# A state-space layer at VectorE's pace: the norm and the batch statistics move to ScalarE and TensorE

## The chip, the cores and the metric

The kernel runs on one core of a Trainium2 chip. A core has five engines that work side by side, each through its own list of instructions in order: TensorE (PE, with its weight loads shown apart as PEld), VectorE (DVE), ScalarE (ACT), GpSimd (POOL) and SyncE (SP), which here issues the transfers. They meet only through semaphores. The metric is the device time of one execution in microseconds.

## The reference

A network of four layers works on an image batch of 4 x 96 x 64 x 64. The change lies in layer 0, two Mamba blocks one after the other with a batch norm at the end:

```python
for i in range(2):
    mu  = seq.mean(-1); var = ((seq - mu) ** 2).mean(-1)
    h   = (seq - mu) * rsqrt(var + EPS) * ln_g + ln_b          # the norm over the 96 channels
    xs, z = split(h @ in_w)
    xc  = silu(causal conv of 4 taps over xs)
    dt, Bm, Cm = split(xc @ xproj_w)
    delta = softplus(dt @ dt_w + dt_b)
    dA, dBx = exp(delta * A), delta * Bm * xc                   # 192 channels x 16 states
    hstates = scan over the tokens of (h = dA * h + dBx)
    y   = (sum over states of hstates * Cm + Dp * xc) * silu(z)
    seq = seq + y @ out_w
out = fus_w @ [seq, pooled] + fus_b
out = (out - mean(out)) * rsqrt(var(out) + EPS) * bn_g + bn_b   # per channel, over batch and pixels
```

Layers 1 to 3 (a convolution block, an attention and a Fourier block with small feed-forward parts) are the same before and after.

## The kernel before

The tokens of each image, 4096, are cut into 4 stretches of 1024. An *item* is one image, one stretch and one of the two blocks, 32 items in all, ordered so that each image's state is carried from stretch to stretch (`items`: stretch, then block i, then image b, so four items of block 0 alternate with four of block 1).

An item has 24 *tiles* of 128 x 1024, each 4 states of 32 channels. For each tile ACT makes dA (`exp`, L455), DVE makes u = delta·xc·B (L471) and the scan (L475), POOL multiplies with C (`times_c`, L481), and PE sums over the states into `y` (`sum_y`, L500). The tiles of `pool_tiles` = 2, 5, 7, 10, 13, 15, 18, 21 divide the work otherwise: POOL makes u (`times_b`, L461), and ACT writes dA into PSUM (`dap`). For the other tiles PE spreads B's rows over the partitions (`rep`, L195: operand x, while u goes to a second buffer). All of x, u and `dap` share one ring of two PSUM buffers (`psum_x`), so `rep` and `dap` of a tile wait until the one or two tiles before are through on DVE.

The order is written out by hand: under `manual_schedule` each engine executes its instructions in the order in which the loop over m (one step for a tile, called a slot below) names them. In a slot stand, in this order: the scan, `rep` or `exp` for the next tile, `exp` three tiles ahead, `times_c`, `keep_state`, `times_b`, the y work, `load_x`, `project`, `finish`, `keep_stats`, and last what `first_stage` has put into the slot. `first_stage(k)` prepares item k while the items before it are scanned; its slot numbers are relative, and modulo 24 they say in which slot of a phase (24 tiles) its work stands. What matters here, with lines:

- slot 13 (-11): item's x is loaded, POOL puts the 3 tokens of the item before into `n` (L266, L268)
- slot 17 (-7): PE subtracts the channel mean with a 96 x 96 matrix `center` (L274), channels on the partitions
- slot 18 (-6): ACT squares (L280) and copies to `n` (L281)
- slot 19 (-5): PE sums the squares over the channels with `ones` (L287), which also spreads the sum over the partitions
- slot 20 (-4): ACT makes the reciprocal root by Ln and Exp (L292, L293)
- slot 21 (-3): DVE multiplies it into `n` (L299), POOL keeps the last 3 tokens (L301)
- slots 22 to 1: matmuls of the convolution from `n` (`spread`, L205), slots 0, 1, 3: ACT copies them out (L309), then Silu
- slot 12: softplus of delta on ACT (L357), with a load of its function table before and one after it (L222)
- slots 12, 13, 13: three matmuls for z (L205, w_z); slots 13, 14, 14: ACT copies them out (L309); slot 19: Silu of z (L383), with two table loads
- the item that has just been scanned: slot 15 `project` (L518, L219) on PE, slot 17 `finish` on ACT (L527 for block 0, L529 for block 1), slot 18 `keep_stats` on DVE (L537, two bn_stats, block 1 alone)

The PSUM tiles of `tile_ps` (L274, L287, the convolution, z, delta, `project`) share another ring of two buffers. A matmul into such a tile waits until ACT has emptied the tile two before it.

Of the kernel before, what the change touches and what calls it, by code (L numbers as in the profile page):

```python
# [9 lines left out]
F32 = mybir.dt.float32  # L10
# [3 lines left out]
AF = mybir.ActivationFunctionType  # L14
ALU = mybir.AluOpType
# [3 lines left out]
B, C, HW, L = 4, 96, 64, 4096  # L19
NT = B * L  # L20
T = 1024
NSC = L // T
MB = 512
# [27 lines left out]
class Net:  # L51
# [20 lines left out]
    def consts(self, ctx):  # L72
        tc, nc, ins = self.tc, self.nc, self.ins
        pool = ctx.enter_context(tc.tile_pool(name="const", bufs=1))
        self.cpool = pool
        self.vec = pool.tile([C, NV96], F32, name="vec")
        nc.sync.dma_start(self.vec, ins["vec96"])
        self.vec128 = pool.tile([128, NV128], F32, name="vec128")
        nc.sync.dma_start(self.vec128, ins["vec128"])
        self.ones = pool.tile([C, C], F32, name="ones")  # L80
        nc.vector.memset(self.ones, 1.0)
        self.eps = pool.tile([128, 1], F32, name="eps")
        nc.vector.memset(self.eps, EPS)
# [4 lines left out]
        self.stats = pool.tile([C, NT // MB, 6], F32, name="stats")  # L88
        self.osc = pool.tile([C, 1], F32, name="osc")
        self.osh = pool.tile([C, 1], F32, name="osh")  # L90


    def layer0(self, dram, scratch):
        tc, nc, ins = self.tc, self.nc, self.ins
        x_in = ins["x"]
        with ExitStack() as ctx:
            cp = ctx.enter_context(tc.tile_pool(name="l0c", bufs=1))
# [17 lines left out]
            w_z = cp.tile([C + 1, 2, DIN], F32, name="w_z")  # L115
# [11 lines left out]
            gpw = load(cp, "gpw", [C, C])  # L127
            nega = cp.tile([128, 48], F32, name="nega")
            fbias = cp.tile([C, B], F32, name="fbias")
            pooled = cp.tile([C, B * NSC], F32, name="pooled")  # L130

            with tc.tile_pool(name="l0s", bufs=1) as wk:
# [9 lines left out]
                for a in range(0, 2 * 4 * DIN, MB):  # L142
                    ps = small(C + 1, MB)
# [6 lines left out]
                for i in range(2):  # L150
# [4 lines left out]
                    ps = small(C + 1, HID)  # L155
# [33 lines left out]
            def tile_ps(rows=C):  # L189
                return psum.tile([128, MB], F32, name="ps", tag="ps")[:rows]  # L190
# [54 lines left out]
            def load_x(b, s, i):  # L245
                x = wk.tile([C, T], F32, name="x", tag="x", bufs=2)
                nc.sync.dma_start(x, xd[:, b] if i else x_in[b, :, s * T : (s + 1) * T])
                return x

            def first_stage(k):  # L250
# [5 lines left out]
                def at_slot(t):  # L256
                    def keep(f):
                        steps.setdefault(t - 24, []).append(f)

                    return keep  # L260

                @at_slot(-11)
                def _():
                    m["xn"] = load_x(b, s, i)
                    if s == 0:
                        nc.gpsimd.memset(n[:, :3], 0.0)  # L266
                    else:
                        nc.gpsimd.tensor_copy(n[:, :3], halo[:, b, i])  # L268

                @at_slot(-7)  # L270
                def _():
                    m["ps"] = [tile_ps(), tile_ps()]
                    for at, ps in zip(halves, m["ps"]):
                        nc.tensor.matmul(ps, self.center, m["xn"][:, at], start=True, stop=True)  # L274

                @at_slot(-6)
                def _():
                    m["sq"] = wk.tile([C, T], F32, name="sq", tag="sq")
                    for at, ps in zip(halves, m["ps"]):
                        nc.scalar.activation(m["sq"][:, at], ps, AF.Square)  # L280
                        nc.scalar.copy(n[:C, 3 + at.start : 3 + at.stop], ps)  # L281

                @at_slot(-5)
                def _():
                    m["ps"] = [tile_ps(), tile_ps()]
                    for at, ps in zip(halves, m["ps"]):
                        nc.tensor.matmul(ps, self.ones, m["sq"][:, at], start=True, stop=True)  # L287

                @at_slot(-4)
                def _():  # L290
                    for ps in m["ps"]:
                        nc.scalar.activation(ps, ps, AF.Ln, scale=1.0 / C, bias=self.eps[:C])  # L292
                        nc.scalar.activation(ps, ps, AF.Exp, scale=-0.5)  # L293

                @at_slot(-3)
                def _():
                    for at, ps in zip(halves, m["ps"]):
                        x = n[:C, 3 + at.start : 3 + at.stop]
                        nc.vector.tensor_mul(x, x, ps)  # L299
                    if s < NSC - 1:  # L300
                        nc.gpsimd.tensor_copy(halo[:, b, i], n[:, T:])  # L301

                def parts_of(name, ws, rhs, slots, bufs):

# [52 lines left out]
                    nc.scalar.activation(m["delta"], m["delta"], AF.Softplus)  # L357
                    exp_set()

                parts_of("z", [(w_z[:, i], 3)], n, ((12, 13), (13, 14), (13, 14)), 3)  # L360

                @at_slot(13)
                def _():
# [14 lines left out]
                for p in range(3):  # L378
                    at_slot(14 + 3 * p)(lambda p=p: du(p))

                @at_slot(19)
                def _():
                    nc.scalar.activation(m["z"], m["z"], AF.Silu)  # L383
                    exp_set()
# [148 lines left out]
            def keep_stats(k):  # L533
                b, s, i = items[k]
                a = b * L + s * T
                for at in halves:
                    nc.vector.bn_stats(self.stats[:, (a + at.start) // MB, :], made[k]["x"][:, at])  # L537


            b_slots = {2: 5, 4: 7, 7: 10, 9: 13, 12: 15, 15: 18, 18: 21, 23: NTL + 2}  # L540
# [1 line left out]
            with tc.manual_schedule(engines=engines):  # L542
                gp = global_pool()
                stages = [first_stage(k) for k in range(len(items))]
                first = min(stages[0])
                for m in range(first, last + 19):
                    k, t = divmod(m, NTL)
                    if 0 <= m < last:
                        scan(m, *xu)
                    if 0 <= m + 1 < last:  # L550
                        if on_pool(m + 1):
                            exp(m + 1)
                        elif (t + 1) % NTL in group_starts:
                            xu = rep(m + 1)
                    if 0 <= m + AHEAD < last and not on_pool(m + AHEAD):
                        exp(m + AHEAD)
                    if 1 <= m <= last:
                        times_c(m - 1)
                    if 3 <= m < last + 3:
                        keep_state(m - 3)  # L560
                    if -1 <= m and t in b_slots and m - t + b_slots[t] < last:
                        times_b(m - t + b_slots[t])
                    for k0 in range(max(k - 1, 0), min(k + 1, len(items))):
                        at = m - NTL * k0
                        for p in range(3):
                            if at == 8 * p + 3:
                                start_y(k0, p)

                            if at - 8 * p in (4, 6, 8, 10):
                                sum_y(k0, at - 4)  # L570
                            if at == 8 * p + 11:
                                gate(k0, p)
                        if at == 34:
                            made[k0]["x"] = load_x(*items[k0])
                        if at == 39:
                            project(k0)
                        if at == 41:
# [844 lines left out]
```

## Time and profile before

The time is 4223.3 us, the median of 3 runs (4220.02 to 4226.23). Layer 0 ends at about 2724 us of the profiled 4222.8. Busy time from 200 to 2600 us, the steady part of layer 0:

| engine | busy us of 2400 | share |
|---|---|---|
| POOL | 2288.6 | 95% |
| DVE | 2283.8 | 95% |
| PE | 1745.9 | 73% |
| ACT | 1579.2 | 66% |

The instructions that the change touches, over the whole layer (count by mean duration):

| line | engine, what | count | ns |
|---|---|---|---|
| L274 | PE, centre, records of 96x512 | 128 | 643 |
| L280, L281 | ACT, square and copy, 96x512 | 64 each | 598, 580 |
| L287 | PE, sum of squares | 128 | 620 |
| L292, L293 | ACT, Ln and Exp, 96x512 | 64 each | 644, 574 |
| L309 z | ACT, z's copies, 128x512 | 96 | 580 |
| L383 | ACT, Silu of z, and table loads | 32 | 1486, 1283 each load |
| L529 | ACT, finish of block 1 | 32 | 673 |

In such a table the time of a PE instruction is a record of the profile; a matmul in f32 leaves two records. The durations contain the time in which an instruction overlaps its neighbour, so the distance of two starts is shorter: two copies of 0.58 us start 0.48 us apart.

### The profile page before, as it was taken

The numbers are of one execution on the slowest core, as the hardware profiler recorded it, in microseconds if no ns is written. First come the engines' busy times: TensorE is split into PE (matmuls) and PEld (weight loads), VectorE is DVE, ScalarE is ACT, GpSimd is POOL, SyncE is SP. The second block draws the span as 40 slices with busy tenths as digits, with TensorE's granted clock in tenths as the row PEclk, the third lists the DMA queues.
The fourth block names the chain that finished last, engine by engine and source line by source line (L and its number), as shares of the span: only waits on it lengthen the run. The fifth ranks groups of instructions, "written<-read, shape, count | busy, mean of one in ns | idle before, by whom it ended". The sixth has DMA issues, their size and how long they took to land. (4 is left out here: it accounts for less than half of the span.)

```text
span 4222.8 us, 42511 instructions
## 1 busy us (share of the span) xinstructions
PE 3233.2 (77%) x13088; PEld 1310.8 (31%) x13088; DVE 3189.6 (76%) x2474; ACT 2514.7 (60%) x4098; POOL 2997.8 (71%) x1651
## 2 busy tenths in 40 slices
PE   6677677777767777776777776579999888887987
PEld 2111112111211211121121111277445436555642
DVE  4999999999999999999999999731222583444649
ACT  4666666666666666666666665322555575544547
POOL 1999999999999999999999999611110264333418
PEclk8788888888878888888888887669999998899989
DMA  7557566566656656665665666363000000001111
GB/s 171 136 149 172 132 155 162 139 147 158 164 136 152 161 137 147 161 161 137 151 161 137 147 158 165 77 202 130 0 0 1 1 1 5 23 28 28 44 43 53
DMA packets 183276, 468.02 MB, mean 111 GB/s; under 512 B 53108, under 2 KB 55134, under 8 KB 179968
## 3 DMA queue, kind: packets, MB, share of 16 engines
q1 hardware_dynamic: 183048, 465.31, 43.6%
q8 instruction: 103, 1.69, 0.2%
q14 instruction: 125, 1.02, 0.1%
HBM read 391.62 MB, written 73.50 MB: 110 GB/s over the span
## 5 line engine op out<-in xcount | busy, mean ns | idle before, releaser
L481 POOL TENSOR_TENSOR hs<-hs,crep 128x1024 f32<-128x1024 f32 x768 | 1799.2, 2359 | 108.1 <-DVE hs L475 55.0
L475 DVE TENSOR_TENSOR_SCAN hs<-da,state,u 128x1024 f32<-128x1024 f32 x384 | 901.7, 2348 | 24.9 <-DVE u L471 0.5
L455 ACT ACTIVATE dap<-ddb,nega 128x1024 f32<-128x1024 f32 x256 | 286.3, 1118 | 722.0 <-DVE u L471 721.6
L471 DVE TENSOR_TENSOR u<-udb,rep 128x1024 f32<-128x1024 f32 x512 | 627.7, 1226 | 72.3 <-PE rep L195 40.2
L455 ACT ACTIVATE da<-ddb,nega 128x1024 f32<-128x1024 f32 x512 | 583.7, 1143 | 67.7 <-DVE hs L475 65.7
L195 PE MATMUL rep<-r,sel_bq 96*128 96x512 bf16 x576 | 226.8, 485 | 514.4 <-DVE hs L475 505.9
L461 POOL TENSOR_TENSOR up<-udb,brep 128x1024 f32<-128x1024 f32 x256 | 605.3, 2365 | 4.7 <-DMA ud<-du 4.7
L500 PE MATMUL y<-hs,sel_r 128*32 128x512 f32 x3072 | 501.9, 724 | 4.6 <-POOL hs L481 4.6
L475 DVE TENSOR_TENSOR_SCAN hs<-dap,state,up 128x1024 f32<-128x1024 f32 x192 | 447.1, 2329 | 16.4 <-ACT dap L455 16.4
L205 PE MATMUL ps<-n,w_x 97*64 97x512 f32 x1536 | 424.7, 680 | 10.9 <-DVE n L299 10.8
L475 DVE TENSOR_TENSOR_SCAN hs<-da,u 128x1024 f32<-128x1024 f32 x128 | 293.0, 2289 | 8.1
L195 PEld LDWEIGHTS <-sel_bq 96*128 96x128 bf16 x576 | 39.1, 103 | 780.2 <-DVE hs L475 582.2
L1002 POOL CAST hq<-y 128x512 fp8e5<-128x512 f16 x192 | 118.5, 641 | 222.1 <-DVE y L1001 222.1
L205 PEld LDWEIGHTS ps<-n,w_x 97*64 97x64 f32 x1536 | 152.2, 155 | 287.3 <-issue 217.6
L205 PE MATMUL ps<-n,w_z 97*64 97x512 f32 x384 | 121.1, 714 | 129.3 <-ACT z L309 116.2
L1150 POOL TENSOR_TENSOR av<-av,ec 128x780 f32<-128x780 f32 x32 | 58.8, 1838 | 197.3 <-ACT av L1147 197.3
L796 POOL TENSOR_TENSOR xc<-xc,rs 96x512 f32<-96x512 f32 x32 | 40.4, 1266 | 209.8 <-ACT rs L795 163.8
L500 PEld LDWEIGHTS y<-hs,sel_r 128*32 128x32 f32 x3072 | 65.6, 116 | 319.1 <-issue 167.8
L219 PE MATMUL ps<-xc,xproj 64*102 64x512 f32 x384 | 152.1, 952 | 3.5 <-ACT xc L320 3.5
L475 DVE TENSOR_TENSOR_SCAN hs<-dap,up 128x1024 f32<-128x1024 f32 x64 | 145.3, 2270 | 7.6 <-ACT dap L455 5.7
L373 POOL TENSOR_TENSOR du<-delta,xc 128x512 f32<-128x512 f32 x96 | 122.6, 1277 | 32.1 <-ACT delta L357 22.3
L1147 ACT ACTIVATE av<-xr_ps,vec 128x65 f32<-128x65 f32 x384 | 117.0, 424 | 47.5 <-PE xr_ps L1135 47.5
(255 smaller groups left out, 6067.3 us busy)
## 6 DMA issues: line engine op xcount, KB each, us to landing
ddb<-dd SPq DMA_DIRECT2D x768, 128.0 KB, 3.3
udb<-ud SPq DMA_DIRECT2D x768, 128.0 KB, 4.4
crep<-cd SPq DMA_DIRECT2D x512, 128.0 KB, 4.0
brep<-cd SPq DMA_DIRECT2D x256, 128.0 KB, 3.6
dd<-delta SPq DMA_DIRECT2D x64, 384.0 KB, 3.9
ud<-du SPq DMA_DIRECT2D x192, 128.0 KB, 3.2
band<-in_band SPq DMA_DIRECT2D x24, 1024.0 KB, 4.8
gt<-in_idft SPq DMA_DIRECT2D x64, 256.0 KB, 2.7
```

The costliest lines, as they stand in the source:

```text
L195: nc.tensor.matmul(ps[:, at], w, rhs[:, at_in], start=start, stop=stop, **kw)
L205: nc.tensor.matmul(ps[rows], w[:, 64 * p : 64 * p + 64], rhs[:, at.start + shift : at.stop + shift], start=k == 0, stop=k == len(ws) - 1, ...
L219: nc.tensor.matmul(ps, w[rows, p], x[rows, p], start=start and p == 0, stop=p == 2)
L373: nc.gpsimd.tensor_mul(u, m["delta"][:, of], m["xc"][:, of])
L455: nc.scalar.activation(da, made[k]["dd", h, j], AF.Exp, scale=nega[:, col : col + 1])
L461: nc.gpsimd.tensor_mul(u, made[k]["ud", h, j], made[k]["brep", g])
L471: nc.vector.tensor_mul(u, made[k]["ud", h, j], x)
L475: nc.vector.tensor_tensor_scan(hs[:, 1:], made[k].pop(("da", t)), u, 0.0 if s == 0 else st, ALU.mult, ALU.add)
L481: nc.gpsimd.tensor_mul(hs[:, :T], hs[:, 1:], made[k]["crep", order[t][1]])
L500: nc.tensor.matmul(made[k]["y", p][row : row + 32], sel_r, made[k]["hs", t][:, at], start=False, stop=True, skip_group_check=True,)
L1002: nc.gpsimd.tensor_copy(q[:, m, :], y2, saturate=False)
L1147: nc.scalar.activation(v[:, k, d], xr[:, at], AF.Identity, scale=self.v128(w, cg + d), bias=self.v128(bias, cg + d))
```

## The change

The norm is made with the tokens on the partitions. PE takes pieces of 128 tokens of x as the stationary operand and `center` as the moving one, so that the centred values come out as 128 tokens x 96 channels. There the sum of squares over the channels is a sum along the free axis, which ACT's Square gives as its accumulator output; the reciprocal root is one value for each token, on 128 x 8 instead of 96 x 1024, and ACT multiplies it in as a scale for each partition. PE then turns the pieces back with the identity matrix, and ACT copies them into `n`. DVE's multiply is gone; POOL's two small copies of three tokens go to ACT (a memset at the start of each image stays on POOL).

The batch statistics were DVE's bn_stats. Now ACT's `finish` gives the sum of each piece as its accumulator output, and a second ACTIVATE gives the sum of squares, shifted by the mean of the first piece. The end of the layer makes mean and variance of these sums.

To make room on ACT, the copies of z come a slot later (14, 15, 15; the third z matmul in slot 14 instead of 13), and Silu of z moves from slot 19 to 16.

```diff
                 @at_slot(-7)
                 def _():
-                    m["ps"] = [tile_ps(), tile_ps()]
-                    for at, ps in zip(halves, m["ps"]):
-                        nc.tensor.matmul(ps, self.center, m["xn"][:, at], start=True, stop=True)
+                    m["ps"] = [tile_ps(128), tile_ps(128)]
+                    for q in range(8):
+                        nc.tensor.matmul(
+                            m["ps"][q // 4][:, q % 4 * C : q % 4 * C + C],
+                            m["xn"][:, q * 128 : q * 128 + 128],
+                            self.center,
...
                 @at_slot(-6)
                 def _():
-                    m["sq"] = wk.tile([C, T], F32, name="sq", tag="sq")
-                    for at, ps in zip(halves, m["ps"]):
-                        nc.scalar.activation(m["sq"][:, at], ps, AF.Square)
-                        nc.scalar.copy(n[:C, 3 + at.start : 3 + at.stop], ps)
+                    m["nt"] = wk.tile([128, 8, C], F32, name="nt", tag="nt")
+                    m["rs"] = wk.tile([128, 8], F32, name="rs", tag="rs")
+                    for q in range(8):
+                        nc.scalar.activation(
+                            m["nt"][:, q],
+                            m["ps"][q // 4][:, q % 4 * C : q % 4 * C + C],
+                            AF.Square,
+                            accum_out=m["rs"][:, q : q + 1],
+                        )
+                    nc.scalar.activation(m["rs"], m["rs"], AF.Ln, scale=1.0 / C, bias=self.eps)
+                    nc.scalar.activation(m["rs"], m["rs"], AF.Exp, scale=-0.5)
...
                 @at_slot(-5)
                 def _():
-                    m["ps"] = [tile_ps(), tile_ps()]
-                    for at, ps in zip(halves, m["ps"]):
-                        nc.tensor.matmul(ps, self.ones, m["sq"][:, at], start=True, stop=True)
+                    for q in range(8):
+                        x = m["ps"][q // 4][:, q % 4 * C : q % 4 * C + C]
+                        nc.scalar.mul(m["nt"][:, q], x, m["rs"][:, q : q + 1])
...
                 @at_slot(-4)
                 def _():
-                    for ps in m["ps"]:
-                        nc.scalar.activation(ps, ps, AF.Ln, scale=1.0 / C, bias=self.eps[:C])
-                        nc.scalar.activation(ps, ps, AF.Exp, scale=-0.5)
+                    m["ps"] = [tile_ps(), tile_ps()]
+                    for q in range(8):
+                        nc.tensor.matmul(
+                            m["ps"][q // 4][:, q % 4 * 128 : q % 4 * 128 + 128],
+                            m["nt"][:, q],
+                            self.ident,
...
                 @at_slot(-3)
                 def _():
+                    if s == 0:
+                        nc.gpsimd.memset(n[:, :3], 0.0)
+                    else:
+                        nc.scalar.copy(n[:, :3], halo[:, b, i])
                     for at, ps in zip(halves, m["ps"]):
-                        x = n[:C, 3 + at.start : 3 + at.stop]
-                        nc.vector.tensor_mul(x, x, ps)
+                        nc.scalar.copy(n[:C, 3 + at.start : 3 + at.stop], ps)
                     if s < NSC - 1:
-                        nc.gpsimd.tensor_copy(halo[:, b, i], n[:, T:])
+                        nc.scalar.copy(halo[:, b, i], n[:, T:])
...
-                parts_of("z", [(w_z[:, i], 3)], n, ((12, 13), (13, 14), (13, 14)), 3)
+                parts_of("z", [(w_z[:, i], 3)], n, ((12, 14), (13, 15), (14, 15)), 3)
...
-                @at_slot(19)
+                @at_slot(16)
                 def _():
                     nc.scalar.activation(m["z"], m["z"], AF.Silu)
                     exp_set()
...
-                    else:
-                        nc.scalar.activation(o[:, at], ps, AF.Identity, bias=fbias[:, b : b + 1])
+                        continue
+                    a = (b * L + s * T + at.start) // MB
+                    nc.scalar.activation(
+                        o[:, at], ps, AF.Identity, bias=fbias[:, b : b + 1], accum_out=self.sums[:, a : a + 1]
+                    )
+                    if (b, s, at.start) == (0, 0, 0):
+                        nc.vector.tensor_scalar_mul(self.shift, self.sums[:, :1], 1.0 / MB)
+                        nc.vector.tensor_scalar(sbias, fbias, self.shift, None, ALU.subtract)
+                    nc.scalar.activation(
+                        ps, ps, AF.Square, bias=sbias[:, b : b + 1], accum_out=self.squares[:, a : a + 1]
+                    )
...
-                        if at == 42 and items[k0][2]:
-                            keep_stats(k0)
...
-            nc.vector.bn_aggr(mv, self.stats)
+            for k, x in enumerate((self.sums, self.squares)):
+                nc.vector.reduce_sum(mv[:, k : k + 1], x, axis=mybir.AxisListType.X)
+            nc.vector.tensor_scalar_mul(mv, mv, 1.0 / NT)
+            nc.vector.tensor_sub(d, mv[:, :1], self.shift)
+            nc.vector.tensor_mul(d, d, d)
+            nc.vector.tensor_sub(mv[:, 1:2], mv[:, 1:2], d)
```

More of the change, by code (lines that the diff above doesn't have):

```diff
@@ L87, in consts @@
         nc.vector.tensor_scalar_add(self.center, self.ident[:C, :C], -1.0 / C)
-        self.stats = pool.tile([C, NT // MB, 6], F32, name="stats")
+        self.sums = pool.tile([C, NT // MB], F32, name="sums")
+        self.squares = pool.tile([C, NT // MB], F32, name="squares")
+        self.shift = pool.tile([C, 1], F32, name="shift")
         self.osc = pool.tile([C, 1], F32, name="osc")
@@ L129, in layer0 @@
             fbias = cp.tile([C, B], F32, name="fbias")
+            sbias = cp.tile([C, B], F32, name="sbias")
             pooled = cp.tile([C, B * NSC], F32, name="pooled")
@@ L264, in _ @@
                     m["xn"] = load_x(b, s, i)
+                @at_slot(-7)
+                def _():
+                    m["ps"] = [tile_ps(128), tile_ps(128)]
[4 more added lines that the diff above has]
+                            self.center,
+                            start=True,
+                            stop=True,
+                        )
+                @at_slot(-6)
+                def _():
+                    m["nt"] = wk.tile([128, 8, C], F32, name="nt", tag="nt")
[9 more added lines that the diff above has]
+                    nc.scalar.activation(m["rs"], m["rs"], AF.Exp, scale=-0.5)
+                @at_slot(-5)
+                def _():
+                    for q in range(8):
+                        x = m["ps"][q // 4][:, q % 4 * C : q % 4 * C + C]
+                        nc.scalar.mul(m["nt"][:, q], x, m["rs"][:, q : q + 1])
+                @at_slot(-4)
+                def _():
+                    m["ps"] = [tile_ps(), tile_ps()]
[4 more added lines that the diff above has]
+                            self.ident,
+                            start=True,
+                            stop=True,
+                        )
+                @at_slot(-3)
+                def _():
                     if s == 0:
@@ L267, in _ @@
                     else:
-                        nc.gpsimd.tensor_copy(n[:, :3], halo[:, b, i])
-                @at_slot(-7)
-                def _():
-                    m["ps"] = [tile_ps(), tile_ps()]
+                        nc.scalar.copy(n[:, :3], halo[:, b, i])
                     for at, ps in zip(halves, m["ps"]):
-                        nc.tensor.matmul(ps, self.center, m["xn"][:, at], start=True, stop=True)
-                @at_slot(-6)
-                def _():
-                    m["sq"] = wk.tile([C, T], F32, name="sq", tag="sq")
-                    for at, ps in zip(halves, m["ps"]):
-                        nc.scalar.activation(m["sq"][:, at], ps, AF.Square)
-                        nc.scalar.copy(n[:C, 3 + at.start : 3 + at.stop], ps)
-                @at_slot(-5)
-                def _():
-                    m["ps"] = [tile_ps(), tile_ps()]
-                    for at, ps in zip(halves, m["ps"]):
-                        nc.tensor.matmul(ps, self.ones, m["sq"][:, at], start=True, stop=True)
-                @at_slot(-4)
-                def _():
-                    for ps in m["ps"]:
-                        nc.scalar.activation(ps, ps, AF.Ln, scale=1.0 / C, bias=self.eps[:C])
-                        nc.scalar.activation(ps, ps, AF.Exp, scale=-0.5)
-                @at_slot(-3)
-                def _():
-                    for at, ps in zip(halves, m["ps"]):
-                        x = n[:C, 3 + at.start : 3 + at.stop]
-                        nc.vector.tensor_mul(x, x, ps)
+                        nc.scalar.copy(n[:C, 3 + at.start : 3 + at.stop], ps)
                     if s < NSC - 1:
-                        nc.gpsimd.tensor_copy(halo[:, b, i], n[:, T:])
+                        nc.scalar.copy(halo[:, b, i], n[:, T:])
                 def parts_of(name, ws, rhs, slots, bufs):
@@ L527, in finish @@
                         nc.scalar.copy(o[:, at], ps)
-                    else:
-                        nc.scalar.activation(o[:, at], ps, AF.Identity, bias=fbias[:, b : b + 1])
+                        continue
+                    a = (b * L + s * T + at.start) // MB
+                    nc.scalar.activation(
+                        o[:, at], ps, AF.Identity, bias=fbias[:, b : b + 1], accum_out=self.sums[:, a : a + 1]
+                    )
+                    if (b, s, at.start) == (0, 0, 0):
[3 more added lines that the diff above has]
+                        ps, ps, AF.Square, bias=sbias[:, b : b + 1], accum_out=self.squares[:, a : a + 1]
+                    )
                 a = b * L + s * T
                 nc.sync.dma_start(scratch[:, a : a + T] if i else xd[:, b], o)
[L533 to L537, printed above, removed]
             b_slots = {2: 5, 4: 7, 7: 10, 9: 13, 12: 15, 15: 18, 18: 21, 23: NTL + 2}
@@ L588, in layer0 @@
             mv = cp.tile([C, 2], F32, name="mv")
-            nc.vector.bn_aggr(mv, self.stats)
+            d = cp.tile([C, 1], F32, name="bn_d0")
+            for k, x in enumerate((self.sums, self.squares)):
[4 more added lines that the diff above has]
+            nc.vector.tensor_sub(mv[:, 1:2], mv[:, 1:2], d)
             r = self.rsqrt(cp, mv[:, 1:2], "bn_r")
```

## The prediction, made before the changed kernel ran

> **What bounds the kernel now.** First the busy table by stretch of layer 0 (columns: us, then busy us and instructions of PE, PEld, DVE, ACT, POOL, then granted clock, DMA share, GB/s):
>
> ```profile
> 1000.00:1400.00 400.00, 293.89 (x1128) 77.67 (x1130) 383.16 (x227) 263.70 (x410) 382.83 (x182) 0.82 0.61 152
> ```
>
> DVE and POOL are both busy 96% of the stretch; ACT has 136 us of 400 free. So the layer runs at DVE's pace, with POOL a hair behind, and the question is which DVE time is work and which is waiting. The waits of DVE from 200 to 2600 us (engine, line, what it waited for, total, times, longest):
>
> ```profile
> DVE u L471 <- PE rep L195: 32.5, 40, 1.5
> DVE hs L475 <- ACT dap L455: 21.1, 28, 0.9
> DVE u L471 <- DMA ud<-du: 8.1, 6, 1.5
> ```
>
> I numbered the scans in DVE's timeline from 0 to 23 in each item (a scan and what precedes it is a slot; 24 slots make a phase). The norm's multiply L299 stands in slot 21; its starts give the phase: 161.65 to 2538.07 us is 29 phases, 81.9 us each. Over the layer all DVE waits of 30 phases lie in three slots: 15 for dap (22 us), 16 for rep (32 us, with the 8.1 put down to a DMA), 19 for rep (10.4 us). That is about 2.2 us a phase; the other 79.7 us is DVE work. The same place in one phase, DVE, then ACT, then PE (start us, duration, line):
>
> ```profile
> 1036.88 2.35 DVE L475 TENSOR_TENSOR_SCAN hs<-dap,state,up 128x1024 f32<-128x1024 f32 x1 [0.76 <-ACT dap L455]
> 1039.99 1.23 DVE L471 TENSOR_TENSOR u<-udb,rep 128x1024 f32<-128x1024 f32 x1 [0.76 <-PE rep L195]
> ```
> ```profile
> 1034.05 1.15 ACT L455 ACTIVATE da<-ddb,nega 128x1024 f32<-128x1024 f32 x1
> 1035.10 0.17 ACT L488 COPY state<-hs 128x1 f32<-128x1 f32 x1
> 1035.18 0.58 ACT L309 COPY z<-ps 128x512 f32<-128x512 f32 x1
> 1035.66 1.12 ACT L455 ACTIVATE dap<-ddb,nega 128x1024 f32<-128x1024 f32 x1
> ```
> ```profile
> 1035.81 1.32 PE L205 MATMUL ps<-n,w_z 97*64 97x512 f32 x4 [3.68 <-ACT z L309]
> 1037.06 1.93 PE L500 MATMUL y<-hs,sel_r 128*32 128x512 f32 x8
> 1038.92 1.03 PE L195 MATMUL rep<-r,sel_bq 96*128 96x512 bf16 x2
> ```
>
> The third z matmul needs the PSUM buffer that ACT's first z copy frees; rep queues behind it on PE, and DVE behind rep.
>
> **What the skill says.** The Trainium skill, "ScalarE: Activation LUTs", section What ACT_TABLE_LOAD costs: an ACTIVATE takes 186 ns + 0.833 N, 93 ns more for each per-partition pointer, and neighbours overlap by 93 ns. The trace agrees: a 97x96 copy took 243 ns, a 512 copy 578 ns (starts 0.48 us apart), with a bias pointer 673. "TensorE: Matmul & The Clock Gate", Part 1: an idle window of some 3.4 us halves PE's clock. The trace nearly agrees: after idle of up to 2.46 us the matmuls ran at full rate, after 3.05 to 3.14 us rep took 1.03 instead of 0.60 us. "SBUF — State Buffer", Who interferes with whom: a DVE instruction with two SBUF inputs contends with POOL's reads. L299 has one input in PSUM, and L481 takes 2359 ns on the mean beside all of this, so I expect POOL's instructions to stay as long.
>
> **The change part by part.**
>
> *The norm's multiply leaves DVE.* In DVE's timeline L299 pushes the next u by 1.28 us (1060.13 to 1061.41) or 1.18 (1305.94 to 1307.12); DVE does not wait in slots 20 to 23, so all of it counts: 30 phases by 1.23 = **−37 us**. Of POOL go two 0.19 us copies and 17.6 us of waiting for L299; POOL has 3.7 us slack a phase, so this is worth nothing.
>
> *Statistics leave DVE.* bn_stats takes 1.18 us on DVE (1294.92 to 1296.10) in slot 18, in the 16 phases after an item of block 1. In two of them no next norm follows: **−2.4 us**. In 13 rep of slot 19 comes right behind, see the fourth part; the last is in the tail.
>
> *z a slot later.* Call A the end of softplus's table load (1034.05). dap no longer has a 0.48 us copy ahead of it, so slot 15's wait shrinks from 0.76 to about 0.3. But the first z copy now follows da, state, dap, da, state: it ends at A+3.9, and the third z matmul starts then instead of A+1.76. The y matmuls (1.86 us) now stand ahead of it, in time that was idle. So rep comes 2.17−1.86 = 0.3 us later, and later still because PE has now idled 4.8 us instead of 3.7. At half clock the z matmuls take 1.87 us (items where the record reads 1.97), against 1.41 on average now: +0.8. Bounds −0.5 (full clock, rep 0.6) and +0.8; I take +0.6, on 31 phases: **+19 us**. What one wait loses the next gains.
>
> *Squares in finish.* Two ACTIVATEs of 0.58 us become four, plus the accumulator: not in this trace, between 0 and one more small instruction (state's 0.18 us) each; I take 0.1. The centre matmuls of slot 17 wait for finish's PSUM buffers, and rep of slot 19 queues behind them on PE, and u behind rep. Now the buffers come free 0.68 and 1.2 us after finish starts; with Squares after 1.45 and 2.8. The second four centre matmuls take 8 x 0.111 = 0.89 us (the 97x128 transposes of L892: eight records in 0.89), so rep starts at 3.7 and u at 4.4 us after finish's start, against 3.52 (1292.58 to 1296.10) now, where bn_stats was the later one. So +0.9, the removed 1.18 being used up already. With 0.18 us reads it is +1.2. If PE has dropped to half clock (its wait grows from 2.24 to about 3 us, less what a slower projection ahead of it fills), the centre takes 2 x 1.75 and it is +2.6. I take +1.4: 13 phases, **+18 us**. After items of block 0 finish is as before, and eight small centre matmuls take 16 x 0.111 = 1.78 us, as the two now (1.79): 0, say +1 in all.
>
> *ACT's new work.* Eight Squares 8 x (0.15 + 0.1) = 2 us, Ln and Exp 0.6, eight scaled copies 8 x 0.27 = 2.1 (186 + 80 + 93 ns less the overlap), two halo and two n copies 1.3: 6 us, against 4.4 removed. ACT is free 5 us at slot 0 and 27 us a phase, so only bursts count. Silu (4.1 us with both loads) moves to slot 16, where its end meets the time at which dap of slot 18 may start anyway (1044.97). Squares and scales end at about 1055.5, dap of slot 21 can't start before 1055.53, and scan 21 needs it at 1057.89. No wait: 0. The transposes end near 1056.5; rep behind them waits for scan 20 until 1057.98 anyway. n is then ready about 0.5 us later against DVE than now; in 8 phases of 27 rep of slot 0 has no margin, in the others 0.7 to 1.7 us: **+3 us**. First norm and tail (longer chain, six small DVE operations instead of one aggregate): **+2 us**.
>
> Sum: −37 −2.4 +19 +18 +1 +3 +2 = **+3.6**, 4227 us.
>
> **The rivals.** *E, the gain is eaten by PE's queue* (above): 4227, give or take 15. *G, the gain stays*: PE keeps its clock through transposes and y matmuls, so rep of slot 16 comes no later (0), finish costs the lower 0.9 (+12), 2 for the rest: −39.4+12+2, **4198**. For it: PE gets more work in slots 18 to 20, and the z chain differs by only 0.3 us before clock effects. Against: 4.8 us without a matmul. *L, PE falls to half clock in both places*: +0.8 x 31 = 25, +2.6 x 13 = 34, slot 0 9, rest 3: −39.4+71, **4255**, slower. For it: every idle of 3.05 to 3.14 us seen was followed by a slow rep. Against: the projection ahead fills some of that idle.
>
> **How the numbers follow.** E 0.38, G 0.36, L 0.26; E is the likeliest and gives the time. E gives 0.08 faster, 0.20 same (4214.9 to 4231.7), 0.10 slower; G 0.34 and 0.02; L 0.26 slower: together 0.42, 0.22, 0.36. The range goes from G's 4190 to L's 4257; the accumulator's bounds (13 x 0.3 us) lie inside.
>
> **What would show it.** L299 and L537 gone from DVE and no new DVE work: part one. DVE's waits for dap in slot 15 down to a third, those for rep in slot 16 at about 1.9 us: part three; if they are below 1 us, G. Waits for rep in slot 19 of about 2.0 us after items of block 1 and 0.6 after the others; 3.5 and centre records of twice the length mean L. A wait of DVE in slot 18 or 21 for dap, or POOL's L481 at another duration, would mean that I have missed something.

## The result and the profile after

After the change the kernel takes 4238.2 us (median of 4 runs, 4234.3 to 4244.8), the one before on the same chip 4222.2 (4 runs, 4220.0 to 4226.2). The ratio is **1.0038 [1.0021, 1.0056]**: slower by 0.4%. That is 11 us above the predicted 4227 and inside the stated range of 4190 to 4257.

The table by stretch, same columns as before:

```profile
1000.00:1400.00 400.00, 285.46 (x1225) 82.51 (x1226) 369.93 (x209) 277.10 (x538) 378.89 (x171) 0.83 0.60 147
```

DVE is now busy 370 us of 400 where it was 383. The work left DVE as planned, and DVE's waits grew by more than was taken from it. Its waits from 200 to 2600 us:

```profile
DVE u L493 <- PE rep L198: 71.3, 40, 3.0
DVE u L493 <- DMA brep<-cd: 22.1, 10, 2.2
DVE u L493 <- DMA ud<-du: 17.3, 8, 2.3
DVE hs L497 <- ACT dap L477: 7.7, 23, 0.5
```

Waiting for dap fell from 21.1 to 7.7 us. Waiting of u grew, under three names, from 40.6 (rep 32.5, a DMA 8.1) to 110.7. The two DMAs are names only: in all 31 phases rep's last record ends 0.04 us before the u of slot 16 starts. Here is one of the `brep<-cd` waits, in DVE's timeline of the same phase as in the prediction, with PE and ACT beside it (start us, duration, line; idle before and what ended it in brackets):

```profile
1040.35 2.35 DVE L497 TENSOR_TENSOR_SCAN hs<-dap,state,up 128x1024 f32<-128x1024 f32 x1 [0.28 <-ACT dap L477]
1044.91 1.23 DVE L493 TENSOR_TENSOR u<-udb,rep 128x1024 f32<-128x1024 f32 x1 [2.22 <-DMA brep<-cd]
```
```profile
1041.93 1.98 PE L208 MATMUL ps<-n,w_z 97*64 97x512 f32 x4 [4.85 <-ACT z L331]
1043.84 1.03 PE L198 MATMUL rep<-r,sel_bq 96*128 96x512 bf16 x2
1044.67 3.62 PE L540 MATMUL ps<-x,ident 96*96 96x512 f32 x4
```
```profile
1038.00 1.15 ACT L477 ACTIVATE da<-ddb,nega 128x1024 f32<-128x1024 f32 x1
1039.06 0.17 ACT L510 COPY state<-hs 128x1 f32<-128x1 f32 x1
1039.14 1.11 ACT L477 ACTIVATE dap<-ddb,nega 128x1024 f32<-128x1024 f32 x1
1040.19 1.13 ACT L477 ACTIVATE da<-ddb,nega 128x1024 f32<-128x1024 f32 x1
1041.23 0.18 ACT L510 COPY state<-hs 128x1 f32<-128x1 f32 x1
1041.31 0.57 ACT L331 COPY z<-ps 128x512 f32<-128x512 f32 x1
```

Read it backwards from u at 1044.91. Rep ended at 1043.84 + 1.03 = 1044.87; so it was rep that u waited for. Rep stood behind the third z matmul (1.98 us; in the kernel before the same four records took 1.32 here, and 1.08 at full rate), which started at 1041.93, as soon as ACT's z copy ended (1041.31 + 0.57 = 1041.88). The copy comes after da, state, dap, da, state. PE had been idle 4.85 us, and rep and the projection behind it (L540, 3.62 us, where 1.88 is seen below in a run that keeps the rate) are still slow.

The other place is slot 19 of a phase whose finish handles an item of block 1. In the kernel before, finish starts at 1292.58, bn_stats ends after rep, and u follows the scan by 3.42 us:

```profile
1292.68 2.32 DVE L475 TENSOR_TENSOR_SCAN hs<-dap,state,up 128x1024 f32<-128x1024 f32 x1
1294.92 1.26 DVE L537 BATCH_NORM_STATS2 stats<-x 96x6 f32<-96x512 f32 x2
1296.10 1.21 DVE L471 TENSOR_TENSOR u<-udb,rep 128x1024 f32<-128x1024 f32 x1
```

The same phase after the change; PE, ACT, then DVE:

```profile
1291.70 3.62 PE L540 MATMUL ps<-x,fus 96*96 96x512 f32 x4
1295.25 4.63 PE L222 MATMUL ps<-z,fo 64*96 64x512 f32 x12
1301.42 1.13 PE L274 MATMUL ps<-center,x 96*128 96x96 f32 x8 [0.53 <-ACT ps L559]
1302.75 1.13 PE L274 MATMUL ps<-center,x 96*128 96x96 f32 x8 [0.20 <-ACT ps L559]
1303.71 0.59 PE L198 MATMUL rep<-r,sel_bq 96*128 96x512 bf16 x2
```
```profile
1299.92 0.68 ACT L553 ACTIVATE x<-ps,fbias 96x512 f32<-96x512 f32 x1 [0.74 <-PE ps L222]
1300.51 0.19 ACT L553 ACTIVATION_READ_ACCUMULATOR x<-ps,fbias 96x1 f32 x1
1300.60 0.64 ACT L559 ACTIVATE ps<-ps,sbias 96x512 f32<-96x512 f32 x1
```
```profile
1304.35 1.23 DVE L493 TENSOR_TENSOR u<-udb,rep 128x1024 f32<-128x1024 f32 x1 [2.83 <-PE rep L198]
```

The centre runs at full rate here, each four matmuls of it as soon as a Square (L559) has left their buffer: u comes 4.43 us after finish's start. But finish also waited 0.74 us for the projection (L222), which was still at half rate since slot 16. There are 13 phases of this kind. In seven finish did not wait, and from scan to u it is 4.32 to 4.45 us, where before it was 3.36 to 3.42 (once 3.55); in five finish waited 0.68 to 1.01 us, and it is 5.10 to 5.35; in one (finish at 555.93) it waited, yet the slot lost 0.5. The projection (L540 and L222) took 6.9 to 7.4 us in the seven and 8.1 to 8.4 in the five, so the half rate lasted longer there.

**Where the time went, by slots.** The table has the time from each scan to the next, summed over the phases of layer 0, minus the same sum of the kernel before, each from its own profiled run (us; intervals that changed by less than 2 us are left out). "15" is the interval from scan 15 to scan 16, which holds slot 16's u, and so on. The entries of column 17 are one phase alone, the one in which DVE waits for the first sum of the statistics.

| kernel | 14 (dap) | 15 (rep) | 17 | 18 (rep) | 20 (dap) | 21 (norm) | 22, 23 | all |
|---|---|---|---|---|---|---|---|---|
| after | −15.1 | +36.3 | +2.5 | +20.2 | | −31.4 | +2.1 | +15.9 |
| z_back | | +4.7 | +5.3 | +25.7 | | −31.4 | +5.8 | +10.6 |
| stats_back | −15.1 | +36.3 | | +6.3 | | −31.4 | +2.1 | +0.1 |
| z_alone | −15.0 | +35.1 | | +10.7 | | | | +32.3 |
| fill | −15.0 | −4.2 | +6.3 | +60.0 | | −31.4 | +4.3 | +20.5 |
| fill_two | −15.1 | −4.1 | +6.2 | +25.5 | | −31.4 | +7.3 | −10.8 |
| before_fill_two | | −28.9 | | | | | | −27.1 |
| norm_alone | | +8.6 | | +4.7 | | −31.4 | +5.3 | −11.6 |
| squares_late | | +3.7 | | +3.6 | | −31.4 | +5.3 | −17.1 |
| rep_first | −15.1 | +36.6 | +2.6 | −23.3 | +20.2 | −30.9 | +2.1 | −7.3 |
| all_fill_rep | | −28.9 | | −23.3 | +2.3 | −31.4 | +4.6 | −75.0 |

The row of after is the answer in short: 31.4 gained at the norm, 21.2 net lost at z, 20.2 lost behind finish, some 5 elsewhere.

### The profile page after: what moved, and what is told of

It reads as the page before. It is cut to its first block, busy times and chain, and to the rows that moved or that the text cites. A ratio compares the mean times of both kernels' runs of the same rounds, so it can differ in the third digit from the quotient of the medians.

```text
span 4235.0 us, 44766 instructions
## 1 busy us (share of the span) xinstructions
PE 3244.4 (77%) x13856; PEld 1374.2 (32%) x13856; DVE 3134.0 (74%) x2385; ACT 2578.8 (61%) x4882; POOL 2992.8 (71%) x1603
## 5 line engine op out<-in xcount | busy, mean ns | idle before, releaser
L503 POOL TENSOR_TENSOR hs<-hs,crep 128x1024 f32<-128x1024 f32 x768 | 1798.3, 2359 | 143.3 <-DVE hs L497 58.2
L522 PE MATMUL y<-hs,sel_r 128*32 128x512 f32 x3072 | 467.7, 679 | 4.8 <-POOL hs L503 4.8
L208 PE MATMUL ps<-n,w_x 97*64 97x512 f32 x1536 | 383.5, 639 | 6.2 <-POOL n L317 6.0
L208 PE MATMUL ps<-n,w_z 97*64 97x512 f32 x384 | 131.0, 768 | 169.9 <-ACT z L331 152.6
L208 PEld LDWEIGHTS ps<-n,w_x 97*64 97x64 f32 x1536 | 114.7, 147 | 272.2 <-issue 218.3
L222 PE MATMUL ps<-xc,xproj 64*102 64x512 f32 x384 | 149.1, 935 | 3.5 <-ACT xc L342 3.5
```

The costliest lines, as they stand in the source:

```text
L208: nc.tensor.matmul(ps[rows], w[:, 64 * p : 64 * p + 64], rhs[:, at.start + shift : at.stop + shift], start=k == 0, stop=k == len(ws) - 1, ...
L222: nc.tensor.matmul(ps, w[rows, p], x[rows, p], start=start and p == 0, stop=p == 2)
L503: nc.gpsimd.tensor_mul(hs[:, :T], hs[:, 1:], made[k]["crep", order[t][1]])
L522: nc.tensor.matmul(made[k]["y", p][row : row + 32], sel_r, made[k]["hs", t][:, at], start=False, stop=True, skip_group_check=True,)
```

## The experiments

Each is the kernel after with one edit, unless it says before. Kernels of one group ran on one chip beside the kernel before; between chips the latter's median moved (4214.6, 4222.1, 4219.0), so ratios are given.

### z's copies back, and z's copies alone

z_back, on the kernel after (Silu stays in slot 16):

```diff
-                parts_of("z", [(w_z[:, i], 3)], n, ((12, 14), (13, 15), (14, 15)), 3)
+                parts_of("z", [(w_z[:, i], 3)], n, ((12, 13), (13, 14), (13, 14)), 3)
```

z_alone is the reverse edit on the kernel before. Silu's move from slot 19 to 16 is in every kernel that starts from after; it was not tried apart.

> The changed kernel with z's copies and its third matmul back in slots 13, 14, 14 and 13; Silu of z stays in slot 16. Theory Z (the late first z copy holds rep of slot 16, and the long idle of PE ahead of it halves its clock): the interval from scan 14 to scan 16, 0.68 us longer than before in 31 phases, goes back (-21 us), and the slower projection behind it too (0.37 us in 16 phases, -6): about 4211 us, below the kernel before. Rival A (the new ACT bursts, with Silu in slot 16, delay dap): the time stays near 4238. Rival P (PE's small matmuls of the norm cost it): it stays near 4238 too, with DVE's waits in slot 19.

> The kernel before with one thing changed: z's third matmul in slot 14 and its copies in slots 14, 15, 15; Silu of z stays in slot 19, norm and statistics as before. Theory Z: slot 15's wait for dap falls to 0.28 us, rep of slot 16 comes 0.7 us later than before, projection runs at half clock: +21 us, and up to 6 more for slot 19 after items of block 0: about 4246 us. Rival A (only together with the norm's ACT work does the shift cost): within 5 us of before, about 4222, or faster by the 15 us of dap's wait.

z_alone: 4250.1 us, **1.0086 [1.0071, 1.0100]**. The later copies cost by themselves what the row of after shows for them, −15.0 + 35.1, and +10.7 in slot 19 besides, in a kernel without a Square in finish. ACT's waits from 200 to 2600 us show where from; L527 and L529 are the two lines of finish, L219 the projection:

```profile
ACT x L529 <- PE ps L219: 5.2, 6, 1.0
ACT x L527 <- PE ps L219: 4.0, 5, 1.0
```

The kernel before has no such wait. The slow stretch that begins at z reaches finish, 9.2 us in 11 phases.

z_back: 4229.2 us, **1.0038 [1.0023, 1.0054]**, the same ratio as after. The expected 4211 did not come. The loss of slot 16 is gone (+36 became +5), but with it went the 15 us gained at dap, and other slots lose more than in after: slot 19 in block-1 phases +1.89 us each instead of +1.25. By the table 5 us of the 21 are left, by the medians none. Its PE in a block-1 phase:

```profile
1292.12 2.21 PE L540 MATMUL ps<-x,fus 96*96 96x512 f32 x4
1294.26 2.82 PE L222 MATMUL ps<-z,fo 64*96 64x512 f32 x12
1301.00 1.13 PE L274 MATMUL ps<-center,x 96*128 96x96 f32 x8 [2.93 <-ACT ps L559]
1302.33 1.44 PE L274 MATMUL ps<-center,x 96*128 96x96 f32 x8 [0.20 <-ACT ps L559]
1303.57 1.06 PE L198 MATMUL rep<-r,sel_bq 96*128 96x512 bf16 x2
```

The projection is quick again (2.82 instead of 4.63), so PE runs dry and idles 2.93 us ahead of the centre; during the centre the clock falls (1.44 us for the second eight records instead of 1.13) and rep takes 1.06 instead of 0.59. In after the slow projection had filled that idle. So this is rival L's second half, met in the kernel in which the first half was mended.

### The statistics back on DVE, and the norm alone

stats_back gives finish its old form again:

```diff
-                    nc.scalar.activation(
-                        o[:, at], ps, AF.Identity, bias=fbias[:, b : b + 1], accum_out=self.sums[:, a : a + 1]
-                    )
...
-                    nc.scalar.activation(
-                        ps, ps, AF.Square, bias=sbias[:, b : b + 1], accum_out=self.squares[:, a : a + 1]
-                    )
+                    else:
+                        nc.scalar.activation(o[:, at], ps, AF.Identity, bias=fbias[:, b : b + 1])
...
+                        if at == 42 and items[k0][2]:
+                            keep_stats(k0)
...
+            nc.vector.bn_aggr(mv, self.stats)
```

norm_alone is this and z_back's edit together: of the change only the norm and Silu's slot are left.

> The changed kernel with the statistics as before: bn_stats on DVE, no accumulators and no Squares in finish. Theory S (the Squares hold the PSUM buffers for which the centre matmuls wait, and rep of slot 19 behind them): the interval from scan 18 to scan 19 after items of block 1, now 1.25 us longer than before, comes to within 0.1 us of before although bn_stats is on DVE again: -15 us in 13 phases, +2 in the last two, about 4225 us. Rival: that interval is long because of the norm's eight small matmuls: then bn_stats adds its 1 us and the time rises to about 4250.

> Only the norm's part of the change (with Silu of z in slot 16): z's slots and the statistics as in the kernel before. Theories Z and S together (the norm's part gains, the other two parts lose): -31 us of DVE work, +5 for slot 16, +3 for slot 19 after items of block 0, +6 for the rest: about -17 us, ratio 0.996. Theory P (the norm's small matmuls and ACT's bursts eat its gain): ratio 1.000 or above, with longer waits in slots 18 to 21.

stats_back: 4217.6 us, **1.0004 [0.9995, 1.0014]**; block-1 phases lose 0.14 us in slot 19 instead of 1.25, block-0 phases 0.28 instead of 0.37. With the Squares in finish, moving the statistics to ACT was a loss, and most of it lies in those 13 phases. norm_alone: 4204.5 us, **0.9955 [0.9940, 0.9970]**: of 31.4 us gained 11.6 are left in the layer by the table, with losses in slots 16, 19, 23 and 0; the medians differ by 17.6.

### Is it the clock? Matmuls with a zero weight

`none` is a tile of zeros; the added matmuls add zero to a y that is being accumulated. fill puts four of them into slot 14, fill_two two more into slot 17 (its edit is shown); before_fill_two puts the same into slots 13 and 17 of the kernel before.

```diff
+            none = cp.tile([128, 128], F32, name="none")
+            nc.vector.memset(none, 0.0)
...
+                        if at in (14, 17):
+                            for _ in range(4 if at == 14 else 2):
+                                nc.tensor.matmul(
+                                    made[k0]["y", 1], none, made[k0]["xc"][:, 1], start=False, stop=True, skip_group_check=True
+                                )
```

> The changed kernel with work for PE in its longest gap: four matmuls of 128x512 with a weight of zeros, added to the open y sums in slot 14 behind the y matmuls, about 3.4 us at full clock. They add nothing to the result. Theory C (half clock after the idle): the third z matmul then takes 1.0 instead of 1.9 us, rep 0.6 instead of 1.0, the projection 4.8 instead of 7.0: DVE's wait in slot 16 falls from 2.2 to about 0.9 us and slot 19 is as before after items of block 0: 31 x 1.3 + 6, about 4190 us. Rival O (the wait comes from the order of ACT's copies alone): slot 16 keeps its 2.2 us and the time stays at 4238 or rises by what the fillers take on PE.

> The changed kernel with fillers of zero weight in both gaps of PE: four matmuls in slot 14 ahead of z's third matmul, and two in slot 17 ahead of the centre matmuls. Theory C (half clock): with one filler slot 16's wait fell from 2.2 to 0.9 us, but PE then idled 2.7 to 3.5 us ahead of the centre matmuls, whose 16 records took up to 3.7 us instead of 2.0, and the loss came back in slot 19. With both fillers the centre runs at full clock: against the kernel before the intervals from scan 14 to 16 stay at -19 us, scan 18 to 19 comes to 0 after items of block 0 and +0.9 us after those of block 1 (12 us), the norm's multiply gives -31: about -36 us, ratio 0.9915. Rival O (what comes back in slot 19 is the time of the extra matmuls on PE or ACT's Squares, not the clock): slot 19 keeps its 1.7 and 2.7 us or gets worse, ratio about 1.006.

> The kernel before with the same fillers (slot 13, as its third z matmul stands there, and slot 17) and nothing else. Theory C: the z matmul and rep of slot 16 run at full clock, DVE's wait in slot 16 (31.6 us in all) falls to nearly nothing, slot 15's wait for dap (22 us) stays, slot 19 stays (its centre ran at full clock already): -28 us, ratio 0.9935. Rival O: no gain, or a loss by the fillers' time on PE (2 x 0.85 us in slot 17, ahead of rep of slot 19): ratio 1.000 to 1.006.

fill: 4236.5 us, **1.0062 [1.0044, 1.0080]**, no gain at all, where about 4190 was expected. Its PE says why; L603 is the filler, L276 the centre. First one phase, then the centre of the next:

```profile
1043.88 3.70 PE L603 MATMUL y<-xc,none 128*128 128x512 f32 x8
1048.80 1.08 PE L210 MATMUL ps<-n,w_z 97*64 97x512 f32 x4 [1.22 <-ACT z L333]
1049.81 0.61 PE L200 MATMUL rep<-r,sel_bq 96*128 96x512 bf16 x2
1050.25 1.88 PE L542 MATMUL ps<-x,ident 96*96 96x512 f32 x4
1058.55 2.02 PE L276 MATMUL ps<-center,x 96*128 96x96 f32 x16 [2.67 <-ACT x L551]
1060.41 0.84 PE L200 MATMUL rep<-r,sel_bq 96*128 96x512 bf16 x2
```
```profile
1139.68 3.73 PE L276 MATMUL ps<-center,x 96*128 96x96 f32 x16 [2.67 <-ACT x L551]
1143.20 1.06 PE L200 MATMUL rep<-r,sel_bq 96*128 96x512 bf16 x2
```

In slot 16 the clock is kept: z 1.08 instead of 1.98, rep 0.61 instead of 1.03, the projection (L542) 1.88 instead of 3.62. Slot 16's +36.3 fell to −4.2. But with the projection done early PE idles 2.67 us ahead of the centre. In the first of these two phases the centre still runs at full rate (2.02 us) and only rep behind it is slow in part; in the next, after the same idle, the centre takes 3.73 us. Over the whole kernel the centre's records have, in after and in fill (ns, minimum/median/maximum):

```profile
L274 PE MATMUL ps<-center,x x512: 274/276/529, 25.5 to 2543.4; 96*128 96x96 f32 x171
L276 PE MATMUL ps<-center,x x512: 275/421/530, 25.1 to 2548.8; 96*128 96x96 f32 x171
```

Slot 19 lost 60 us. Two more fillers in that idle (fill_two) bring this down to 25.5; the first of the two phases again:

```profile
1050.32 2.02 PE L276 MATMUL ps<-center,x 96*128 96x96 f32 x16 [0.76 <-ACT x L551]
1052.18 0.59 PE L200 MATMUL rep<-r,sel_bq 96*128 96x512 bf16 x2
```

fill_two: 4209.8 us, **0.9970 [0.9959, 0.9981]**, about a third of the expected gain. The same fillers give the kernel before 4185.9 us, **0.9913 [0.9899, 0.9927]**: its wait for rep goes from 32.5 us to

```profile
DVE u L473 <- PE rep L197: 10.6, 18, 0.8
```

with nothing else changed but idle time of PE. What is left is the wait of slot 19 (10.4 us before); in slot 16, where u waited 31.6 us, it no longer waits at all (in the phase of 1018.41 z takes 1.08 us and rep 0.60). So that wait was PE's clock, not the order of its work. The table accounts for 27 of the 36 us between the medians; in the profiled run the first scan also came 6 us earlier, which varies from run to run.

The fair pair is fill_two against before_fill_two: both keep their clock in slot 16, and the change is still 24 us slower (medians). By the table: −31.4 at the norm; +9.7 at z (−15.1 − 4.1, where before_fill_two has −28.9), which is left to the late copy itself; +25.5 in slot 19; +13.5 in slots 17, 23 and 0; together 17 of the 24. In slot 19 finish starts 0.06 to 0.35 us after the scan (before: 0.03 to 0.18 ahead of it, once 0.45), and in about half of the block-1 phases the end of the centre or rep is slow still. The trace shows why finish starts later: in all phases but one ACT has no idle time from z's third copy to finish, and Silu with its two table loads (1043.43 to 1047.50 in the phase above) now stands between them, while ACT idled 4.7 to 5.8 us there in the kernel before. So it is Silu's new slot that holds finish back here; another slot for it was not tried.

### Squares in an empty slot, and rep ahead of the centre

squares_late keeps all that relieves DVE, with z's slots as before. finish has only its Identity (with the sum); the Squares read x in SBUF five slots later.

```diff
+            def squares(k):
+                for at in halves:
...
+                    nc.scalar.activation(
+                        junk, made[k]["x"][:, at], AF.Square, bias=sbias[:, :1], accum_out=self.squares[:, a : a + 1]
+                    )
...
+                        if at == (42 if k0 == len(items) - 1 else 46) and items[k0][2]:
+                            squares(k0)
```

rep_first is the kernel after, with the centre matmuls a slot later, so that rep of slot 19 is issued ahead of them:

```diff
-                @at_slot(-7)
+                @at_slot(-6)
```

> The changed kernel with z's slots as before, and with the Squares of the statistics taken out of finish: they read the finished x in SBUF, in slot 22, where ACT has time, so that finish gives the PSUM buffers free after its two Identity instructions. All of DVE's relief stays. Theories Z and S: -31 us for the norm, slot 19 after items of block 1 at -0.2 us against before, as DVE now waits for rep there instead of doing bn_stats (-3), -2 for the last two phases, +5 and +3 as in the run with z's slots alone, +6 for the rest: about -22 us, ratio 0.995. Rival: two more ACTIVATEs in slot 22 delay xc's copies and rep of slot 0: ratio about 1.000.

> The changed kernel with its eight centre matmuls named in slot 18 instead of 17, behind rep of slot 19 instead of ahead of it; nothing else. Theory S (rep of slot 19 is late only because it queues on PE behind matmuls that wait for finish's Squares): DVE's wait in slot 19 goes altogether, 46.6 us in the changed kernel. Against the kernel before: +21 for z's slots, -31 for the norm, -10 after items of block 0, -15 for bn_stats, +5 for the rest: about -30 us, ratio 0.993. Rival N (the norm's chain has no slack: centre later means n later, and rep of slot 0 behind the convolution's matmuls): a new wait in slot 0 or at dap of slot 21, ratio about 1.000.

squares_late: 4202.7 us, **0.9948 [0.9931, 0.9966]**. Slot 19 loses 3.6 us, against 25.7 in z_back, which has z's slots as before too, but the Squares in finish; the layer gains 17.1. The Square itself is nearly free; its place ahead of the centre was not. But norm_alone, which leaves bn_stats on DVE, took 4204.5 us on the same chip: even with the Squares well placed, moving the statistics shows no gain beyond the noise, as DVE waits for rep there anyway. It pays where rep stands ahead of the centre: in the next run the block-1 phases gain 0.98 us each.

rep_first: 4215.6 us, **0.9988 [0.9980, 0.9996]**, a gain over after, but not the expected 0.993: nearly half of slot 19's 43 us (+20.2 to −23.3) is lost again in slot 21 (+20.2 where after had none), which is where rival N looked. DVE's wait for dap:

```profile
DVE hs L497 <- ACT dap L477: 21.2, 40, 1.0
```

It is back at 21.2 us from 7.7: with the centre late, ACT's Squares and scales of the norm come late too, and dap of slot 21 stands behind them. The slot that the norm's chain was given had no slack.

### All of these

all_fill_rep is squares_late with the centre in `at_slot(-6)`, four fillers in slot 13 and two in slot 17.

> All that the runs have shown together: the changed kernel with z's slots as before, the Squares in slot 22 from SBUF, centre in slot 18 behind rep, and fillers of zero weight in slots 13 and 17 that keep PE's clock. Theories Z, S and C: -31 us for the norm, -29 for slot 16, -10 and -15 for slot 19, +6 for the rest; slot 15's wait for dap (22 us) stays: about -79 us, ratio 0.981. Rival (POOL, with 3.7 us of slack in a phase before, becomes the bound, and DVE waits for it): ratio 0.985 to 0.99, with waits for hs or up of POOL on DVE.

4143.1 us (4135.4 to 4146.8), **0.9815 [0.9801, 0.9828]**: faster than both kernels. Its waits and its stretch:

```profile
DVE hs L499 <- ACT dap L479: 23.1, 30, 1.0
DVE u L495 <- DMA ddb<-dd: 1.6, 1, 1.6
```
```profile
1000.00:1400.00 400.00, 305.63 (x1350) 93.93 (x1346) 385.05 (x218) 282.60 (x549) 390.73 (x177) 0.90 0.63 156
```

Of the waits for rep one is left (1.6 us; it is put down to a DMA, but rep ends 0.04 us before this u starts), otherwise only that for dap in slot 15. The gain (75 us) is more than the sum of squares_late (17.1) and the fillers (about 27 in the kernel before): rep ahead of the centre, which in rep_first paid in slot 21, is nearly free (+2.3) once Squares are out of finish and PE keeps its clock; which of the two frees it was not tried apart. POOL, busy 391 of 400 us, is now busier than DVE (385), though DVE does not wait for it yet.

## Why the prediction came out as it did

The mechanism was right: what DVE no longer does, it waits for PE's queue. In the terms of the prediction:

- **The norm's multiply: −37, measured −31.4.** The working took how far L299 pushes the next u. It left out that scan 21 followed directly by u needs 2.43 us from start to start, and followed by L299 only 2.24. From scan to u it was mostly 3.42 to 3.52 us and is 2.43, 1.0 to 1.1 us a phase, and no wait has come in its place (the lines stand below). bn_stats is the same: −0.97 in each of the two phases where no next norm follows, not −1.2.
- **z a slot later: +19, measured +21.2** (−15.1 and +36.3). dap's wait went to 0.28, the copy ended at A + 3.9 (A = 1038.00), PE idled 4.85 us, z took 1.98 and rep 1.03, each as worked out.
- **Squares in finish: +1.4 a phase, measured +1.25 (16 of the +20.2), by another mix, so that the sizes meet is luck.** From finish's start to u it is 4.4 us, as worked out for a clock kept, and the seven phases in which finish did not wait lose the 0.9 to 1.1 that follows. The half-rate centre, which was to bring the rest, did not come. What did is finish's wait for the half-rate projection, which makes it 1.6 to 2.0 in five phases. The working took the slow projection only as something that fills PE's idle time, not as something that ACT waits for.
- **Block 0: +1, measured +6.** The same omitted step: three phases in which finish waited 0.69 to 0.75 us lose 1.2, 1.1 and 0.5; in four more, which lose 0.45 each, the centre stood behind the slow projection. z_alone and stats_back lose 0.38 and 0.28 us a phase here, without Squares.
- **Slot 0: +3, measured +0.7**, all of it in the first five phases. The +2.1 in the table lie a slot earlier: in slot 23 the scan starts 0.07 us later behind its u in each phase, without a wait; why is not known.
- **First norm and tail: +2**; seen are 2.5 in slot 17, DVE's wait for the first sum that sets `shift` (once 1.5 us) and its small operations. The first scan came 1.9 us earlier.

The slot of the norm's multiply in one phase, before and after:

```profile
1057.89 2.33 DVE L475 TENSOR_TENSOR_SCAN hs<-dap,state,up 128x1024 f32<-128x1024 f32 x1
1060.13 1.35 DVE L299 TENSOR_TENSOR n<-n,ps 96x512 f32<-96x512 f32 x2
1061.41 1.22 DVE L471 TENSOR_TENSOR u<-udb,rep 128x1024 f32<-128x1024 f32 x1
```
```profile
1062.91 2.33 DVE L497 TENSOR_TENSOR_SCAN hs<-dap,state,up 128x1024 f32<-128x1024 f32 x1
1065.34 1.23 DVE L493 TENSOR_TENSOR u<-udb,rep 128x1024 f32<-128x1024 f32 x1
```

Sum of the layer: 14.0 us by the last scan (2718.6 against 2704.6), +3.6 predicted. About 6 of the missing 10 are the multiply's size, 5 block 0.

Of the rivals, G fell: its premise, that PE keeps its clock in slot 16, is what the 4.85 us idle took away. Keeping it by other means (fill_two) does bring the change below the kernel before, but the same means bring that kernel further. L is right for slot 16 and wrong for slot 19 in this kernel, since the slow projection fills the gap; z_back and fill show it there.

As to the Trainium skill, "TensorE: Matmul & The Clock Gate", Part 1: the idle window of some 3.4 us that it gives is longer than what these runs show. After idle of 2.67 us (fill) and 2.93 us (z_back) matmuls already ran slow, in part or in whole. The prediction read in the kernel before that after idle of up to 2.46 us all ran at full rate. It overlooked two phases, those with idle of 2.29 and 2.46 us, in which the centre nearly did so, but rep behind it took 1.06 instead of 0.59 us:

```profile
1949.53 2.02 PE L274 MATMUL ps<-x,center 96*96 96x512 f32 x4 [2.46 <-ACT x L529]
1951.35 1.06 PE L195 MATMUL rep<-r,sel_bq 96*128 96x512 bf16 x2
```

That idle can end in half rate is confirmed, 1.98 against 1.08 us for the same four records. But the length of the one idle stretch does not decide it alone: in the kernel before, the third z matmul took 1.08 us after idle of 3.58 us (at 789.75) and 1.98 after 3.59 us (at 2184.97). The price of an ACTIVATE that the prediction takes from "ScalarE: Activation LUTs", What ACT_TABLE_LOAD costs, gives as an estimate 266, 612 and 705 ns where the trace has 243, 578 and 673, so it agrees within a tenth and is too high each time.

## What to carry to other kernels

When PE is the queue and not the bound, its clock is still part of each wait: price an idle stretch of PE by what may run slow after it, and follow the slow stretch to all who wait behind it, not only to the first. When one gap is mended, look for the next: work that finishes sooner leaves PE dry elsewhere, and cheap matmuls that add zero gave the kernel before 0.9% without moving any work. And before work is moved from a busy engine to a free one, look at what stands behind its new place: slot 19 lost 26 us with the Squares ahead of the centre and 4 with the same Squares in an empty slot.

## What the runs showed of the hardware

The accumulator output is an instruction of its own (ACTIVATION_READ_ACCUMULATOR), 0.19 us long, but it moves the next start by only 0.09 us (1300.51 to 1300.60). Over the layer's norms it takes 0.22 us on the mean, beside 0.26 for the Square of 128x96.

The half rate lasted well beyond the idle: after 4.85 us idle at 1041.93, z, rep and L540 ran slow up to 1048.3, and in the block-1 phase L222 too. It need not begin with the first matmul after the idle either (the centre at full rate, rep behind it slow). POOL's L503 kept its 2359 ns through all of it. What stays open: what decides when the clock falls (after idle of 2.3 to 3.6 us both rates were seen, and in fill_two rep took 0.98 us at 1298.19 after idle of only 1.62 and 0.20 us around the centre), and whether the last dap wait, 22 us of slot 15, can be had with the z copies where they were.
